# Fifteen quarter products for six tiles of fc1's second half, and new paces for the convolutions, in a two-block image kernel

## The chip, the cores and the metric

The kernel runs on one core of one Trainium2 chip. All arithmetic is in 32-bit floats. The metric is the device time of one execution in microseconds (us); the median over the runs counts.

The engines are TensorE (PE in the profile, PEld for its weight loads), VectorE (DVE), ScalarE (ACT), GpSimd (POOL) and SyncE (SP). Each engine takes its own instructions in the order in which they were issued to it. PE writes its results into PSUM banks, which VectorE and ScalarE read.

## The reference

The input is 8 images of 384 channels and 32 x 32 positions, so 1024 tokens. Each goes through two blocks; what follows is the arithmetic with the set-up left out.

```python
# block 0: attention and MLP, 8 heads of 48, on tokens (N = 1024, C = 384)
xn  = layernorm(xf, eps=1e-5) * g1 + beta1
q, k, v = split(xn @ w_qkv.T + b_qkv)
out = softmax(q @ k.T * 48**-0.5) @ v
x1  = out @ w_proj.T + b_proj + xf
xn2 = layernorm(x1, eps=1e-5) * g2 + beta2
h   = gelu(xn2 @ w_fc1.T + b_fc1)            # 384 -> 1536
y   = x1 + h @ w_fc2.T + b_fc2               # 1536 -> 384
# block 1: 7 x 7 depthwise convolution, MLP with global response norm
z   = depthwise_conv(y, dw_w, pad=3) + dw_b
z   = layernorm(z, eps=1e-6) * ln_w + ln_b
z   = gelu(z @ w1 + b1)                      # 384 -> 1536
gx  = sqrt(sum over positions of z**2); nx = gx / (mean(gx) + 1e-6)
z   = gamma * (z * nx) + gbeta + z
out = y + z @ w2 + b2                        # 1536 -> 384
```

## The kernel before, in words

**Layout.** Channels lie on the 128 partitions, so 384 channels are 3 tiles and 1536 hidden channels are 12 (HT). Tokens run along the free axis, and a matmul takes a half of them (512 columns, NH) at a time. A product of one 128 x 128 weight block with 512 columns is two matmul instructions in the trace. The images are called 0 to 7 here.

**One image after another.** For each image the program issues q and k (L549), attention (scores L664, products L684, the softmax reciprocals `average` L634 to L651, `proj` L606), the layer norm behind it (L413 to L451, its sums over channels as matmuls with ones at L380 and L394), fc1 and fc2 in `mlp`, and the convolution of block 1 (L998). Block 1's two matmul stages of the image before (L338 and L358, `grn_up` and `grn_down`) run on PE while VectorE does the convolution taps of this one. The last image is split by halves instead (`mlp_by_halves`), and its convolution (`last_convolution`) runs in two parts, image rows 0 to 13 and 13 to 32. Its matmuls come in three pieces of 416, 288 and 320 tokens (`last_up` L1168, `grn_down_straight` L1124).

**The order is written out by hand.** There is no scheduler. An object `flow` keeps a plan clock in microseconds: each matmul adds to it (`flow.pe(U)`, 0.857 for a product of 512 columns), and work for the other engines is written as Python generators that yield how long to wait. When the plan clock passes the due time of a generator, its next instructions are issued, between two matmuls. A generator spawned as "paced" keeps to its own times; another counts on from when it was called. `flow.finish` issues all the rest of one at once. So the plan decides only the order of issue on each engine, and semaphores decide when an instruction runs.

**The convolution.** `convolution` issues one tap (one multiply-add of VectorE over a whole channel tile, 1.16 us in the trace) after another, with a pace in plan microseconds. In images 0 to 6 a second generator, `help_convolution`, does 7 of the 49 taps of each channel tile on ACT and POOL (L1019, L1020), and while it works on a tile, VectorE leaves that one alone. The layer norm of the convolution's output follows when both are done.

**fc1.** `mlp` calls `gelu_half` (L768) for each of 12 tiles of hidden channels, first for the first half of the tokens, then for the second. A tile is three products of 512 columns into one of four single PSUM banks (`linear_half` L351) and a gelu on ScalarE (L370) from the bank into the hidden array `hid`. During the first half, after tile 3, the rest of attention and the layer norm of the second half's tokens are issued; the second half starts when that norm is finished. In the second half VectorE has nothing to do for fc1.

**fc2.** `by_thirds` (from L822) takes the 3 x 3 blocks of the weights by 15 products in place of 18, with sums of weight blocks (`FORMS`) made once, in image 0, by `forms` in `prepare` and stored in DRAM (`s_fc2`, `s_w2` for block 1). Its first sums over `hid` are differences of two halves, made by `difference` (L785 negates on ScalarE, L786 adds by a DMA on POOL's queue) during fc1's second half, after its tiles 3 and 5.

**Weights and banks.** Weights come through a ring of 9 buffers of 128 x 768, loaded by SP's queue in a fixed plan; `weights.used` gives a buffer back and starts the next load (L279). SP's queue also moves the softmax reciprocals to where `average` multiplies by them. PSUM has four single banks (`ps_o`) and two double ones (`ps_s`), each set handed out in turn.

Of the kernel before, what the change touches and what calls it, by code (L numbers as in the profile page):

```python
# [51 lines left out]
P = 128  # L52
# [12 lines left out]
CM = 2  # L65
NC = HT // CM
U = 0.857
HELPED = 7
SCALE = HD ** -0.5
EPS0, EPS1, GRN_EPS = 1e-5, 1e-6, 1e-6  # L70
# [81 lines left out]
def block_kernel(  # L152
# [25 lines left out]
    flow = Flow()  # L178
    quiet = []
    s_fc2 = dram.tile([P, len(FORMS), 4 * P], F32, tag="s_fc2", bufs=1, name="s_fc2")  # L180
    s_w2 = dram.tile([P, len(FORMS), 4 * P], F32, tag="s_w2", bufs=1, name="s_w2")
    s_qk = dram.tile([P, CT, 4 * P], F32, tag="s_qk", bufs=1, name="s_qk")
    s_w1 = dram.tile([P, HT // 2, 4, P], F32, tag="s_w1", bufs=1, name="s_w1")

    def half(h):
        return slice(h * NH, (h + 1) * NH)
# [103 lines left out]
    def chunk(w, c):  # L290
        return w[:, c * 6 * P : (c + 1) * 6 * P]
# [1 line left out]

    RAW = ("A11", "A12", "A21", "A22", "A31", "A32")

    def plan_fc1(tag):
        return [((f"fc1_{tag}", c), chunk(wfc1, c)) for c in range(NC)]

    def plan_fc2(tag):
        return [((f"fc2_{tag}", a), chunk(wfc2, c)) for c, a in enumerate(RAW)]  # L300
# [1 line left out]
    def block_of(w, m, k):  # L302

        at = ((m - 1) * HT + 4 * (k - 1)) * P
        return w[:, at : at + 4 * P]
# [8 lines left out]
    def plan_fc2_fast(tag):  # L314
        return plan_thirds(f"fc2_{tag}", wfc2, s_fc2)
# [467 lines left out]
    def difference(dst, more, less):  # L783

        nc.scalar.mul(dst, less, -1.0)  # L785
        nc.gpsimd.dma_start(out=dst, in_=more, accum_op=ALU.add)  # L786
# [5 lines left out]
    def add_first(xt, r, n, bank):  # L792
        dst = xt[:, r, half(n)]
        nc.vector.scalar_tensor_tensor(dst, bank, col("bfc2", r), dst, ALU.add, ALU.add)

    def mlp(b, xt, xn, weights, tag, ln, rest, before_fc2=None, behind_ln=None):

        hid = one.tile([P, HT * N], F32, tag="big", name=f"hid_{b}").rearrange("p (m n) -> p m n", m=HT)
        e = [three.tile([P, 2, NH], F32, tag="p", name=f"fc2_e_{b}_{i}") for i in range(2)]
        wa = f"fc1_{tag}"  # L800
        flow.finish(ln)
        for m in range(HT):
            gelu_half(hid, m, 0, xn, weights, wa, f"fc1_{b}")
            if m == 3 and rest:
                rest()
                slow = 1.2 if b == 1 else 1.0
                ln = flow.spawn(layernorm(xt, xn, 1, eps0, "g2", f"ln2_{b}", True, slow=slow))
                behind_ln(ln)
        flow.finish(ln)
        for m in range(HT):  # L810
            gelu_half(hid, m, 1, xn, weights, wa, f"fc1_{b}")
            if m % CM == CM - 1:
                weights.used(wa, m // CM)
            if m in (3, 5):
                two_tiles = hid[:, m - 3 : m - 1, :]
                difference(e[(m - 3) // 2], two_tiles[:, :, half(0)], two_tiles[:, :, half(1)])
        if before_fc2:
            before_fc2()
        bias = lambda r: col("bfc2", r)
        by_thirds(xt, hid, e, True, weights, f"fc2_{tag}", bias, lambda r, n: pad_half(xt, r, n), f"fc2_{b}")  # L820
# [458 lines left out]
    def prepare(weights, aside):  # L1279
# [17 lines left out]
        def load_blocks(w, name, *which):  # L1297
            t = one.tile([P, CT, N], F32, tag="acc", name=name).rearrange("p c n -> p (c n)")
            parts = []
            for j, (m, k) in enumerate(which):  # L1300
                parts.append(t[:, j * 4 * P : (j + 1) * 4 * P])
                nc.gpsimd.dma_start(out=parts[j], in_=block_of(w, m, k))
            return parts

        def spare(name):
            return three.tile([P, NH], F32, tag="res", bufs=4, name=name)
# [4 lines left out]
        def add(dst, x, y):  # L1311
            nc.vector.tensor_tensor(dst, x, y, ALU.add)

        def forms(name, w, store):
            def keep_form(i, t):
                nc.gpsimd.dma_start(out=store[:, i, :], in_=t)

            a11, a12, a31, a33, a13, a23 = load_blocks(w, f"{name}_a", (1, 1), (1, 2), (3, 1), (3, 3), (1, 3), (2, 3))
            x, y, z = (spare(f"{name}_{k}") for k in "xyz")
            yield 16.0  # L1320
            add(a23, a23, a33)
            add(a11, a11, a12)
            keep_form(6, a11)
            sub(a31, a31, a11)
            keep_form(0, a31)
            yield 2.0
            add(x, a11, a13)
            sub(x, x, a23)
            keep_form(8, x)
            nc.vector.scalar_tensor_tensor(y, a11, -1.0, a33, ALU.mult, ALU.subtract)  # L1330
            keep_form(5, y)
            yield 2.0
            sub(z, a23, a12)
            keep_form(11, z)
            sub(a13, a13, a12)
            sub(a13, a13, a33)
            keep_form(13, a13)
            yield 2.0
            nc.vector.tensor_scalar(a12, a12, -1.0, None, ALU.mult)
            keep_form(12, a12)  # L1340
            nc.vector.tensor_scalar(a23, a23, -1.0, None, ALU.mult)
            keep_form(14, a23)
            a21, a22, a31, a32, a33, a12 = load_blocks(w, f"{name}_b", (2, 1), (2, 2), (3, 1), (3, 2), (3, 3), (1, 2))
            x, y = spare(f"{name}_v"), spare(f"{name}_w")
            nc.gpsimd.dma_start(out=x, in_=block_of(w, 2, 3))
            yield 25.0
            add(x, x, a33)
            sub(y, a22, x)
            keep_form(7, y)
            add(a12, a12, a21)  # L1350
            add(a12, a12, a31)
            keep_form(9, a12)
            yield 2.0
            add(a22, a21, a22)
            sub(a33, a33, a22)
            keep_form(2, a33)
            add(a22, a22, a31)
            keep_form(4, a22)
            add(a32, a32, a22)
            keep_form(1, a32)  # L1360
# [61 lines left out]
            nc.gpsimd.dma_start(out=s_w1[:, :, int(key[1]) - 1, :], in_=t[:, j])  # L1422
        yield from shift_through_w2()
        yield from forms("w2", w2, s_w2)

    def first_values(xn):

# [10 lines left out]
    def main():  # L1438
# [17 lines left out]
        plan = plan_fc1(0) + plan_fc2_fast(0) + plan_qk(1)  # L1456
        for b in range(1, B):
            if b < B - 1:
                plan += plan_fc1(b) + plan_fc2_fast(b)
            else:  # L1460
                for h in range(2):
                    plan += plan_fc1(f"{b}_{h}") + plan_fc2(f"{b}_{h}")
            plan += plan_w1(b - 1, b < B - 1)
            if b == B - 1:
                plan += plan_w1(f"{b}_0", False)
            plan += plan_w2(b - 1, b < B - 1)
            if b < B - 1:
                plan += plan_qk(b + 1)
# [61 lines left out]
        def last_convolution(h, ct, ln=None):  # L1530
            if ct < 0:
                conv_norm(B - 1, ln)
                next_norms(B - 1)
                return
            ready[h].append(ct)
            if ct == 0:
                rows = (LAST[0].stop // W, H) if h else (0, LAST[0].stop // W)
                conv = convolution(last, 0.86 if h else 0.66, (), *rows, ready[h])
                state["conv"] = flow.spawn(after(state["conv"], conv), paced=True)
                if h == 0:  # L1540
                    state["norm_a"] = flow.spawn(after(state["conv"], last_norm(LAST[0], 2.6)))

        for b in range(B):
# [22 lines left out]
            flow.finish(state["norm3"])  # L1566
            if b < B - 1:
                y, gx = grn_up(b - 1, acc, weights, b - 1)
                start_conv(b, 1.6 if b == B - 2 else 1.65, (26, 2.1), (27, 9.0), (35, 4.4))
                scale = flow.spawn(grn_scale(b - 1, gx, weights, b - 1, y))  # L1570
                next_values(b + 1)
                flow.finish(scale)
                quiet.append("w2")
                grn_down(b - 1, y, xt, weights, b - 1, b - 1)
                quiet.clear()
                xt = load_x(b + 1, "x")
            else:

                norm_b = flow.spawn(after(state["conv"], last_norm(LAST[1], 1.0)))
                norm_c = flow.spawn(after(norm_b, last_norm(LAST[2], 1.2)))  # L1580
                y, gx = grn_up_straight(b - 1, acc, weights, b - 1)
                scale = flow.spawn(grn_scale(b - 1, gx, weights, b - 1))
                flow.finish(state["norm_a"])
                sums = small.tile([P, CT, HT], F32, tag="gx_last", bufs=1, name="gx_last")
                y_last = places()
                last_up(last, y_last, 0, sums, weights)
                flow.finish(scale)
                halves = lambda k, part: y[:, k, part]
                blocks = [(r, half(n)) for r in range(CT) for n in range(2)]
                args = b - 1, halves, kept[b - 1], weights  # L1590
                grn_down_straight(*args, b - 1, b - 1, blocks[:-1])
# [147 lines left out]
```

## Time and profile before

| | |
|---|---|
| Median of 7 runs | 3304.57 us (3303.79 to 3309.61) |
| Profiled execution, its own time | 3305.85 us |
| Its span | 3304.1 us |
| Granted TensorE clock, mean | 0.996 |
| PE busy | 3273.6 us (99%), 14296 matmuls |
| DVE busy | 2396.5 us (73%) |
| ACT busy | 1606.1 us (49%) |
| POOL busy | 484.3 us (15%) |
| fc1's 1152 matmul instructions (L351) | 502.3 us busy |
| Convolution taps of images 0 to 6 (L998 into acc) | 861, 1157 ns each |
| Convolution taps of image 7 (L998 into wqkv) | 288, 697 ns each |

Times in the profile are microseconds of one profiled execution, a mean duration where marked ns. "L351" is line 351 of the kernel, often a helper's. In the order of work, a row has the start, the busy time, engine, line, operation, output and inputs, shape, and the number of equal instructions in a row; a bracket holds the idle time before it and what ended that. PE's matmuls overlap, so the distance between starts, not the duration of one, is what a matmul takes of PE's time.

### The profile page before, as it was taken

Reading aid. Unit: us, or ns where it says so; the run is one execution under the profiler, and the core shown is the slowest. Engines: PE = TensorE matmul, PEld = TensorE weight load, DVE = VectorE, ACT = ScalarE, POOL = GpSimd, SP = SyncE. Lnnn points to the kernel's source line nnn. Section 1 sums busy time; section 2 is a strip of 40 time slices with the busy share of each in tenths; the row PEclk is TensorE's granted clock in tenths of the full one; section 3 lists DMA queues with packets and bytes.
Section 4 is the critical chain, followed back from the end, with each engine's and each line's share of the span. In section 5 each row is a group of like instructions: output and inputs, shape, how many; then the busy total and the mean of one; then the engine's idle time right before and its main releaser. Section 6 shows DMA issues by size and latency. Waiting matters only on the chain.

```text
span 3304.1 us, 38767 instructions
## 1 busy us (share of the span) xinstructions
PE 3273.6 (99%) x14296; PEld 1413.6 (43%) x14296; DVE 2396.5 (73%) x3186; ACT 1606.1 (49%) x2194; POOL 484.3 (15%) x569
## 2 busy tenths in 40 slices
PE   8999999999999999999999999999999999999998
PEld 4344434443344433444344443444434444344455
DVE  4444787887857978579786797767876788879840
ACT  2542663446634375353662636526474355623541
POOL 2121210112110121101211012110221112100000
PEclk9999999999999999999999999999999999999999
DMA  5336732647345563536536373273842647333231
GB/s 197 112 107 144 149 70 71 156 111 158 57 96 143 133 128 56 127 114 164 95 58 143 102 187 71 53 169 89 187 72 59 178 89 173 70 78 89 69 96 43
DMA packets 199109, 368.73 MB, mean 112 GB/s; under 512 B 40768, under 2 KB 46784, under 8 KB 198528
## 3 DMA queue, kind: packets, MB, share of 16 engines
q0 software_dynamic: 80896, 158.63, 26.3%
q1 hardware_dynamic: 117728, 206.83, 21.0%
q8 instruction: 115, 1.88, 0.2%
q10 hardware_dynamic: 288, 0.71, 0.1%
q14 instruction: 82, 0.67, 0.1%
HBM read 187.03 MB, written 34.60 MB: 67 GB/s over the span
## 4 chain that ended last, share of the span: by engine, by line
PE 89%; DMA 1%; issue 0%; DVE 0%; ACT 0%; POOL 0%; POOLq 0%; ACTq 0%; DVEq 0%
PE fc L351 15%; PE s L664 11%; PE o L684 11%; PE h L358 10%; PE fc_p L358 10%; PE o_p L358 9%; PE qk L358 6%; PE o L1124 4%; PE proj L606 3%; PE v L592 3%; PE h_last L1168 2%; PE h L338 2%; PE ln_var L394 1%; PE ln_sum L394 0%; DMA ln_sq<-ln_sq 0%
## 5 line engine op out<-in xcount | busy, mean ns | idle before, releaser
L998 DVE SCALAR_TENSOR_TENSOR acc<-pad,vec,acc 128x870 f32<-128x870 f32 (+7 forms) x861 | 964.2, 1157 | 8.9 <-DMA acc<-tap 4.3
L673 ACT ACTIVATE p<-s 128x1024 f32<-128x1024 f32 x512 | 524.4, 1025 | 285.0 <-PE s L664 278.0
L664 PE MATMUL s<-qk 48*64 48x512 f32 x4096 | 546.1, 592 | 0.2 <-ACT qk L505 0.2
L684 PE MATMUL o<-p,v 64*64 64x512 f32 x4096 | 543.4, 590 | 0.0
L351 PE MATMUL fc<-xn,fc 128*128 128x512 f32 x1152 | 502.3, 594 | 0.0
L1020 POOL DMA_DIRECT2D acc<-tap x294 | 253.5, 878 | 1211.9 <-ACT tap L1019 772.2
L351 PEld LDWEIGHTS fc<-xn,fc 128*128 128x128 f32 x1152 | 217.5, 190 | 280.6 <-issue 268.8
L358 PE MATMUL fc_p<-hid,fc 128*128 128x512 f32 x728 | 319.4, 596 | 0.0
L370 ACT ACTIVATE hid<-fc,bfc_f 128x512 f32<-128x512 f32 x192 | 131.4, 686 | 343.8 <-PE fc L351 343.7
L684 PEld LDWEIGHTS o<-p,v 64*64 64x64 f32 x4096 | 165.4, 133 | 278.4 <-issue 270.1
L664 PEld LDWEIGHTS s<-qk 48*64 48x64 f32 x4096 | 161.6, 133 | 277.7 <-issue 222.9
L358 PE MATMUL o_p<-y,w 128*128 128x512 f32 x624 | 270.9, 592 | 0.0
L1069 DVE TENSOR_TENSOR y<-h,y 128x512 f32<-128x512 f32 x288 | 197.1, 690 | 89.8 <-PE h L358 75.2
L1019 ACT ACTIVATE tap<-pad,vec 128x512 f32<-128x512 f32 x294 | 213.0, 734 | 13.7 <-DMA acc<-tap 13.6
L358 PEld LDWEIGHTS fc_p<-hid,fc 128*128 128x128 f32 x728 | 138.3, 191 | 177.6 <-issue 173.5
L358 PE MATMUL h<-acc,w_A 128*128 128x512 f32 x432 | 207.3, 595 | 0.0
L358 PEld LDWEIGHTS o_p<-y,w 128*128 128x128 f32 x624 | 118.0, 190 | 148.7 <-issue 132.0
L998 DVE SCALAR_TENSOR_TENSOR wqkv<-pad,vec,wqkv 128x377 f32<-128x377 f32 (+24 forms) x288 | 177.4, 697 | 0.6
L625 DVE TENSOR_TENSOR attn<-o,attn 128x512 f32<-128x512 f32 x64 | 44.2, 690 | 164.2 <-ACT attn L623 164.2
L790 ACT COPY pad<-x 128x512 f32<-128x512 f32 x48 | 30.2, 635 | 250.0 <-DVE x L856 194.1
L549 DVE TENSOR_TENSOR qk<-qk,qk 128x512 f32<-128x512 f32 x168 | 114.5, 689 | 37.2 <-PE qk L358 28.6
L592 PE MATMUL v<-wqkv,xn 128*128 128x384 f32 x384 | 128.8, 493 | 0.0
(311 smaller groups left out, 3751.5 us busy)
## 6 DMA issues: line engine op xcount, KB each, us to landing
acc<-tap POOLq DMA_DIRECT2D x294, 256.0 KB, 3.4
w_A<-in_w SPq DMA_DIRECT2D x72, 384.0 KB
fc<-s_fc SPq DMA_DIRECT2D x91, 256.0 KB
hid<-hid POOLq DMA_DIRECT2D x42, 512.0 KB, 7.1
fc<-in_wfc SPq DMA_DIRECT2D x54, 384.0 KB
w<-s_w SPq DMA_DIRECT2D x78, 256.0 KB
y<-y POOLq DMA_DIRECT2D x36, 512.0 KB, 7.2
kept<-x SPq DMA_DIRECT2D x8, 1536.0 KB
```

Of the source, the lines that this page charges most:

```text
L351: nc.tensor.matmul(out=ps, lhsT=lhsT(k), rhs=rhs(k)[:, half(h)], start=(k == 0), stop=(k == nk - 1))
L358: nc.tensor.matmul(out=bank, lhsT=lhsT, rhs=rhs, start=k == 0, stop=k == len(pairs) - 1)
L370: nc.scalar.activation(dst, src, function, **kw)
L592: nc.tensor.matmul(out=ps[:, :C], lhsT=xn[:, k, t * P : (t + 1) * P], rhs=wv_sb[:, k, :], start=(k == 0), stop=(k == CT - 1),)
L664: nc.tensor.matmul(out=s[64 * i : 64 * i + 64, j, :], lhsT=kT[64 * j : 64 * j + HD, m, k0 : k0 + 64], rhs=qT[64 * j : 64 * j + HD, m, half ...
L673: nc.scalar.activation(p, s, AF.Exp)
L684: nc.tensor.matmul(out=outs[i][64 * j : 64 * j + 64, :], lhsT=v[keys, t, at : at + 64], rhs=p[keys, j, :], start=(t == 0), stop=(t == KT - 1),
L998: nc.vector.scalar_tensor_tensor(dst, window, tap, dst, ALU.mult, ALU.add)
L1019: nc.scalar.mul(t.rearrange("p (h w) -> p h w", w=W), window, tap)
L1020: nc.gpsimd.dma_start(out=acc[:, ct, half(h)], in_=t, accum_op=ALU.add)
L1069: nc.vector.tensor_tensor(dst, bank, part, ALU.add)
L1124: nc.tensor.matmul(out=ps, lhsT=tiles[k], rhs=y(k, part), start=(k == 0), stop=(k == HT - 1))
```

## The change

In images 1 to 6 the second half of the tokens in fc1 is taken in another way for hidden tiles 6 to 11. These six are two groups of three tiles (`FAST = 2`). Within a group the 3 x 3 weight blocks (three tiles by three channel tiles) meet the second half of the tokens cut into two quarters of 256 columns, and the six blocks of the result are made from 15 products of 256 columns, where there were 18, by the same forms as in fc2.

- `quarter_sums` makes ten sums of quarters of the tokens on VectorE before the first group, behind the layer norm.
- `fc1_group` issues the 15 products into seven banks (y, t, z, v single; x and three others from the double ones), with a second product added onto the same bank five times, and 13 operations of VectorE and four copies of ScalarE that put the results together. The gelus of a group, on `hid` in place, are kept in the list `late` and issued among the next group's or the next tiles' products.
- The second half goes: tiles 0 and 1, group 0, tile 2, group 1, tile 3, then 4 and 5. The first half begins with tiles 6 to 11, whose weight chunks are given back there. The differences for fc2 are issued with group 0 (tiles 0 and 1) and after tile 3.
- The weights' forms for fc1 (`s_fc1`, 15 forms of two groups) are made and stored in image 0, after those of w2.
- The paces of the convolutions change: 1.65 to 1.58 in images 1 to 5, 1.6 to 1.55 in image 6, and in image 7 0.66 to 0.56 for the first part and 0.86 to 0.72 for the second.

```diff
+FAST = 2
...
+    def plan_fc1(tag, fast=False):
+        order = [*range(NC // 2, NC), *range(NC // 2)] if fast else range(NC)
+        return [((f"fc1_{tag}", c), chunk(wfc1, c)) for c in order]
+
+    def plan_fc1_fast(tag):
...
+            for i, (k, l) in enumerate(((0, 6), (6, 12), (12, 15))):
+                plan.append(((f"fc1f_{tag}", g, i), s_fc1[:, g, k:l, :].rearrange("p i o -> p (i o)")))
...
+    def quarter_sums(xn, t):
+        b11, b12, b21, b22, b31, b32 = (xn[:, k, quarter(n, NH)] for k in range(3) for n in range(2))
+        e, f, h, e2, g, f2, h2, g2, f3, d = t
+        minus = ((e, b11, b12), (f, e, b21), (h, e, b31), (f3, f2, g2), (d, g2, b31))
+        plus = ((e2, h, b12), (g, b22, f), (f2, f, b12), (h2, h, b32), (g2, g, b32))
+        for n, (dst, x, y) in enumerate(minus[:3] + plus + minus[3:]):
+            nc.vector.tensor_tensor(dst, x, y, ALU.subtract if n < 3 or n > 7 else ALU.add)
+            if n % 2:
+                yield 1.0
+
+    def fc1_group(hid, group, xn, sums, weights, wname, name, late):
...
+        def product(i, ps, more=False):
+            w = weights.at(wname, group, i // 6)[:, i % 6, :]
+            nc.tensor.matmul(out=ps, lhsT=w, rhs=right[i], start=not more, stop=True, skip_group_check=more)
+            flow.pe(U / 2)
...
+        y = product(6, bank("y"))
+        nc.scalar.copy(c11, y)
+        t = product(2, bank("t"))
+        nc.scalar.mul(c21, t, -1.0)
+        x = product(0, bank("x", True))
+        nc.scalar.copy(n16, x)
+        z = product(10, bank("z"))
+        product(5, y, True)
+        lately()
+        product(1, t, True)
+        v_ = product(12, bank("v"))
+        nc.scalar.copy(c12, v_)
+        op(n16, y, n16)
+        x = product(3, bank("u", True))
+        op(c32, x, n16)
+        op(c32, c32, z, ALU.subtract)
+        x = product(4, bank("w", True))
+        lately()
+        op(c12, c12, z, ALU.subtract)
+        op(n17, x, n16)
+        op(c31, t, n17)
+        x = product(14, bank("q", True))
+        op(c21, x, c21)
+        product(11, v_, True)
+        op(c11, v_, c11)
+        lately()
+        product(7, z, True)
+        product(13, y, True)
+        op(c12, y, c12)
+        product(8, x, True)
+        op(c11, x, c11)
+        product(9, v_, True)
+        op(n17, v_, n17, ALU.subtract)
+        op(c22, z, n17)
+        op(c21, c21, n17)
...
+        late += [gelu(2), gelu(1), gelu(0)]
...
+        fast = FAST if isinstance(b, int) and b > 0 else 0
...
-        for m in range(HT):
+        for n in range(HT):
+            m = (n + HT // 2) % HT if fast else n
             gelu_half(hid, m, 0, xn, weights, wa, f"fc1_{b}")
...
+                making = flow.spawn(after(ln, quarter_sums(xn, sums), 1)) if fast else None
...
+            plain(0)
+            plain(1)
+            late.append(lambda: difference_of(0))
+            fc1_group(hid, 0, xn, sums, weights, f"fc1f_{tag}", f"fc1_{b}", late)
+            plain(2)
+            fc1_group(hid, 1, xn, sums, weights, f"fc1f_{tag}", f"fc1_{b}", late)
+            plain(3)
+            difference_of(1)
+            for m in (4, 5):
+                plain(m)
+                late.pop(0)()
+            late.pop(0)()
...
         yield from forms("w2", w2, s_w2)
+        yield from forms("fc1", wfc1, s_fc1)
...
-                conv = convolution(last, 0.86 if h else 0.66, (), *rows, ready[h])
+                conv = convolution(last, 0.72 if h else 0.56, (), *rows, ready[h])
...
-                start_conv(b, 1.6 if b == B - 2 else 1.65, (26, 2.1), (27, 9.0), (35, 4.4))
+                start_conv(b, 1.55 if b == B - 2 else 1.58, (26, 2.1), (27, 9.0), (35, 4.4))
```

The names in `fc1_group` with a 1 or 2 behind a c are blocks of the result: "c32" is the third tile's second quarter. `n16` and `n17` are intermediate sums, kept in the two halves of one buffer.

## The prediction

> **What bounds the kernel now.** I read the page first, then the waits of TensorE (PE), then the order of work on PE and VectorE (DVE) in fc1's second half and in the last image. The page says that PE is the path:
>
> ```profile
> PE 3273.6 (99%) x14296; PEld 1413.6 (43%) x14296; DVE 2396.5 (73%) x3186; ACT 1606.1 (49%) x2194; POOL 484.3 (15%) x569
> PE 89%; DMA 1%; issue 0%; DVE 0%; ACT 0%; POOL 0%; POOLq 0%; ACTq 0%; DVEq 0%
> ```
>
> PE idles 30.5 us of 3304.1, most of it at the start. So a matmul taken away is worth its full time, and any new wait of PE costs its full time. The question is what PE will wait for, and DVE at 73% is the candidate. PE in the last image:
>
> ```profile
> 3054.27 0.86 PE L380 MATMUL ln_sum<-ln_a,ones 128*128 128x416 f32 x2
> ...
> 3071.12 24.20 PE L338 MATMUL h<-acc,w_A 128*128 128x512 f32 x56
> 3095.15 7.15 PE L1168 MATMUL h_last<-wqkv,w_A 128*128 128x416 f32 x20
> ...
> 3173.88 0.75 PE L380 MATMUL ln_sum<-ln_a,ones 128*128 128x288 f32 x2 [1.70 <-DVE ln_a L416]
> 3177.07 0.75 PE L380 MATMUL ln_var<-ln_sq,ones 128*128 128x288 f32 x2 [2.44 <-DVE ln_sq L437]
> 3179.44 6.79 PE L1168 MATMUL h_last<-wqkv,w_A 128*128 128x288 f32 x16 [1.62 <-DVE wqkv L451]
> ...
> 3186.61 6.95 PE L1168 MATMUL h_last<-wqkv,w_A 128*128 128x288 f32 x28
> 3193.40 0.70 PE L380 MATMUL ln_var<-ln_sq,ones 128*128 128x320 f32 x2
> ```
>
> Starts give the price of a matmul instruction (each product is two): 512 columns (3095.15 - 3071.12) / 56 = 0.4291 us, 288 columns (3193.40 - 3186.61) / 28 = 0.2425. On the line through both, 256 columns cost 0.2158. The brackets are the waits at the tail of the last convolution: 5.76 us. DVE in the second half of fc1 (image 2, 936.7 to 968.8) and in the last image:
>
> ```profile
> 931.09 11.73 DVE L998 SCALAR_TENSOR_TENSOR acc<-pad,vec,acc 128x930 f32<-128x930 f32 x10
> 942.85 0.69 DVE L413 TENSOR_TENSOR ln_a<-acc 128x512 f32<-128x512 f32 x1
> 943.58 0.69 DVE L416 TENSOR_TENSOR ln_a<-ln_a,acc 128x512 f32<-128x512 f32 x1
> 944.18 0.69 DVE L413 TENSOR_TENSOR attn<-acc 128x512 f32<-128x512 f32 x1
> ...
> 3034.06 10.18 DVE L998 SCALAR_TENSOR_TENSOR wqkv<-pad,vec,wqkv 128x403 f32<-128x403 f32 x19
> 3044.13 1.74 DVE L996 TENSOR_SCALAR wqkv<-pad,vec 128x608 f32<-128x608 f32 x2
> 3045.76 0.61 DVE L413 TENSOR_TENSOR ln_a<-wqkv 128x416 f32<-128x416 f32 x1
> 3046.40 0.59 DVE L416 TENSOR_TENSOR ln_a<-ln_a,wqkv 128x416 f32<-128x416 f32 x1
> ```
> ```profile
> 936.70:968.80 32.10, 32.10 (x82) 13.79 (x81) 12.06 (x16) 11.84 (x18) 4.11 (x4) 1.00 0.39 82
> 2950.00:3044.20 94.20, 94.20 (x231) 40.60 (x230) 91.46 (x171) 25.60 (x36) 2.64 (x4) 1.00 0.34 91
> ```
>
> Columns of the last two: length, then busy time of PE, PEld, DVE, ACT (ScalarE), POOL. In the second half DVE is busy for 12.06 of 32.10 us and ACT for 11.84; nothing there makes DVE wait for PE, so it runs ahead of its plan. In 2950 to 3044, the first part of the last convolution, DVE is full: 91.46 of 94.20.
>
> **Matmuls saved.** A group of three tiles by two quarters took 18 instructions of 0.4291 = 7.72 us and takes 30 of 0.2158 = 6.47: 1.25 less. Two groups in images 1 to 6: 12 x 1.25 = **-15.0 us**. [...] The 288-column row, with a load of 190 ns in each 242, lies where streaming alone puts it, so the sum keeps 15.0; the bounds are 15.0 and, if 256 columns cost as much as 288, 360 x 0.0267 = 9.6 less, which is 5.4.
>
> **What the groups make PE wait for.** DVE had no work of fc1; now it has 13 operations of 256 columns a group, on banks that PE writes again within the group. Behind a product that waits, every later matmul is queued, so each wait counts in full. Price: 512 columns take 0.69, and starts lie 0.60 apart (944.18 - 943.58), or 0.73 where one needs the one before; less 256 columns at 0.96 a ns, which is 0.267: 0.34 and 0.46. Eight and five of these are 5.0 us, beside 6.47 of PE. That fits, just. But DVE takes its queue in order, and the planner puts convolution taps of 1.165 us between. By the code's own pacing the last taps of image 2 stand at plan times 899.5 to 914.1, the second half starts at 901.2 and group 0 (after two plain tiles of 2.57) at 906.3. The pace 1.58 for 1.65 leaves nine taps for ten and ends them at 911.5, no earlier: the last ones wait for the helped channel tile, not for the pace. So seven are done before group 0 needs DVE and two lie inside it. Followed from the group's start (a product 0.43, 0.20 until its result is seen, 0.16 from DVE to PE): c32 is made at 3.65; product 14, which takes the double bank that c32 is read from, waits 0.4 for it; the tap then holds "c12 minus z" back to 5.6, and product 7 on z waits 1.1; product 8 waits 0.3; the second tap holds c12 back to 8.6, and the next plain tile, whose bank is y's, waits 1.0. That is 2.7; group 1, with no tap inside, keeps 0.4 + 0.2 of it: 3.3 an image, 2.3 if only one tap falls inside; I take 2.8, for images 2 to 6. Image 1 keeps the old pace and has four taps in each group (its taps run to plan time 530, the second half to 535): DVE has 4 x 1.165 + 5.0 = 9.7 for the 9.05 of a group and a plain tile, and the same walk gives 3.8. Together 5 x 2.8 + 3.8 = **+17.8**; bounds 3.4 (0.56 an image, no tap ever in the way) and 27. The ten quarter sums (about 3.8 us, DVE) fit before group 0: image 2's DVE has its last xn at 931.1 and group 0 wants its first operation near 944. ScalarE's 24 more copies and moved gelus lie in its 20 us of idle there: 0.
>
> **Moved DMAs.** difference_of(1) moves from 952.9 to about plan tile 10; issue 1.2 and landing near 5.5 us put it 3 us ahead of its product in fc2: 0, and PE pays what it lands later. Chunks 3 to 5 are given back in the first half, so one load of 384 KB goes out on SP ahead of the last softmax reciprocals r (issued 902.2, used 906.0 to 906.7, wanted by proj near 908.3). At queue 1's rate (206.83 MB in 21.0% of the span, 298 GB/s) it takes 1.3 plus 0.35 to issue, against 1.5 of slack: 0.2 x 6 = **+1.0** (0 to 9). The s_fc1 forms add some 20 DVE operations of 0.43 and 28 DMAs on POOL to image 0, after w2's, which end at 242 while the tile they use is wanted at about 340: **+0.5** (0 to 3).
>
> **The denser last convolution.** Its part 1 (147 taps, pace 0.66 to 0.56) ends 147 x 0.10 = 14.7 us earlier in the plan, and with it the layer norm behind it, whose sums PE takes in its order. DVE cannot follow: it is full, and reaches the end at most 1.8 earlier (a tap and one operation less ahead). Before, ln_a was ready at 3046.99 and PE summed it at 3054.27, slack 7.3; now 7.3 - 14.7 + 1.8 - 1.5 (a tap or two of part 2 get in front) = -7.1, so PE waits 7.1 in all there, about 2.3 of it already at the acc norm's variance. Between that sum and the next one, ten taps of part 2, 7.1 us, lie in DVE's queue before it subtracts the mean, while the plan gives it 0.8: the variance's sum waits another 5.7. Part 2 (0.86 to 0.72, 106 us planned for 104 of taps and 9 of other work) ends at 3155 for 3171, and its norm costs 3.1 where 5.76 and some 0.7 at acc's variance went before. 7.1 + 5.7 + 3.1 - 6.5 = **+9.4**; bounds -5.8 (those waits go and none comes) and +14.
>
> **Sum.** -15.0 + 17.8 + 1.0 + 0.5 + 9.4 = +13.7. The profiled execution took 3305.85 (span 3304.1 and 1.75 around it), 1.3 over the median; taken off the median: 3304.57 + 13.7 = **3318.3**.
>
> **Rivals.** *DVE has room where I count none* (faster). One mechanism, DVE's place in its queue against PE's: if it gets to the groups' operations and to the last norm's sums about 7 us earlier than I walk it, the group waits fall to 3.4 and the last image's go: -15.0 + 3.4 + 1.5 - 5.8 = -15.9, 3288.7. For it: DVE idles 20 us in the second half. Against: the 94 us without a gap. It decides where ln_sum's slack stays above 0. *The last convolution costs nothing, the groups what I say*: -15.0 + 17.8 + 1.5 = +4.3, 3308.9; for it, the tail's 5.76 us of waits do shrink. *DVE falls behind for good*: with a tap more in each group (1.165 x 12 = 14) the sum is 3332; for it image 1's 9.7 against 9.05, against it that taps end at 911.5. *It doesn't save matmul time* (256 costs 288's price): +9.6, 3327.9.
>
> **How the numbers follow.** Forecast 0.56, in 3311 to 3328; the two dearer cases 0.04 each, to 3333. Costless last convolution: 0.12, within 0.2% (6.6 us, about what a measurement of this kernel can tell from no change). DVE with room: 0.24, anywhere from 3280 to 3298. Slower by over 0.2%: 0.64; within: 0.12; faster: 0.24. The range leaves out the lower two thirds of the fast case (0.16) and 0.04 at the top: 3292 to 3333.
>
> **What would show it.** Right: PE's matmul count up by 12 x 12 = 144 (14296 to 14440); 256-column starts 0.216 apart; PE waiting about 3 us a second half on DVE, in group 0 more than in group 1; ln_sum of 128x416 waiting on DVE ln_a; the 288-column waits gone or moved. Wrong: second halves 2.5 us shorter (groups free), no wait at ln_sum, a new wait on fc_e or on weights, or PE waits above 25 us in the six images.

## The result, and the profile after

The changed kernel takes 3313.73 us (median of 15 runs, 3311.3 to 3316.45), the kernel before 3304.57 (35 runs): a ratio of 1.0026, 95% interval 1.0019 to 1.0033. It is slower by 9.2 us; the forecast was 13.7 slower. Its profiled execution took 3312.3 us, with a span of 3310.5.

The page of the changed kernel, in the two rows that were shown of before:

```profile
PE 3266.9 (99%) x14440; PEld 1452.3 (44%) x14440; DVE 2478.7 (75%) x3422; ACT 1617.4 (49%) x2240; POOL 504.6 (15%) x597
DVE 7%; PE 4%; DMA 0%; issue 0%; ACT 0%; DVEq 0%
```

There are 144 matmuls more, as forecast, and PE is busy for 6.7 us less; yet the span is longer, so PE waits more. The chain that ended last now leads back to VectorE's taps (its shares add up to 11%: it is followed back through the last image only). PE in the last image, where before had three waits, of 1.70, 2.44 and 1.62 us, all at the 288-column norm:

```profile
2975.86 5.39 PE L361 MATMUL fc<-xn,fc 128*128 128x512 f32 x12 [2.09 <-DVE acc L433]
2982.27 10.66 PE L361 MATMUL fc<-xn,fc 128*128 128x512 f32 x24 [1.03 <-DVE x L804]
...
3049.07 1.08 PE L390 MATMUL ln_sum<-ln_a,ones 128*128 128x416 f32 x2 [4.28 <-DVE ln_a L426]
3049.94 17.24 PE L348 MATMUL h<-acc,w_A 128*128 128x512 f32 x36
3070.59 1.76 PE L390 MATMUL ln_var<-ln_sq,ones 128*128 128x416 f32 x2 [3.42 <-DVE ln_sq L447]
3072.14 40.41 PE L348 MATMUL h<-acc,w_A 128*128 128x512 f32 x92
...
3160.19 0.72 PE L390 MATMUL ln_sum<-ln_a,ones 128*128 128x288 f32 x2 [0.15 <-DVE ln_a L426]
```

The waits have moved from the 288-column norm to the 416-column one, over 100 us earlier, and two new ones stand in fc1 of the last image's second half. The starts of the same work on PE, before and after, say what each stage costs (each line is the difference of two starts in the trace):

| stage on PE | before, us | after, us | difference |
|---|---|---|---|
| start to fc2 of image 0 | 272.97 | 272.08 | -0.9 |
| fc2 of image 0 | 59.20 | 62.01 | +2.8 |
| fc1 and second proj of image 1 | 71.34 | 73.09 | +1.7 |
| fc1 after proj in images 2 to 6, each | 54.44 | 54.21 | -0.23 |
| image 7, from the second proj to the end of fc2 | 112.53 | 116.02 | +3.5 |
| first stage of image 6's block 1, with the 416-column norm's sums in it | 63.20 | 74.63 | +11.4 |
| first piece of image 7's block 1 | 25.36 | 26.89 | +1.5 |
| from there to the end of the other pieces | 99.80 | 90.77 | -9.0 |

What lies between these stages adds -0.2 in all, so PE is 9.7 us later at the last stage. The profile ends only 6.4 us later (3310.5 for 3304.1): from the start of that last stage to the end of the program the changed kernel takes 3.4 us less. Its matmuls there take the same time; behind them GpSimd's last long instruction, the DRAIN at the program's end that the other engines' last ones come after, is shorter. Before and after (shortest, middle and longest of three in ns, then the starts):

```profile
L1735 POOLq DRAIN  x3: 51/107/6679, 3296.6 to 3303.8; - x3
L1886 POOLq DRAIN  x3: 51/107/3739, 3305.6 to 3309.9; - x3
```

The longest one falls by 2.9 us, and the instruction just ahead of it on GpSimd (INC_SWDGE_SEM) by 0.7. So the stages account for 6.4 of the medians' 9.2; the profiled run of before is 1.3 us above its median and that of after 1.4 below, which is the rest. The first row is not the change's: between the profiles below, with the same code there, it differs from before's by between 1.3 us less and 1.0 more.

Then a group. PE and VectorE in group 0 of image 2, in order of time:

```profile
949.03 0.59 PE L838 MATMUL fc_w<-fc_t,fc1f 128*128 128x256 f32 x2
949.71 0.70 PE L838 MATMUL fc_q<-hid,fc1f 128*128 128x256 f32 x2
950.25 0.59 PE L838 MATMUL fc_v<-hid,fc1f 128*128 128x256 f32 x2
951.56 0.70 PE L838 MATMUL fc_z<-hid,fc1f 128*128 128x256 f32 x2 [0.72 <-DVE hid L843]
952.10 0.59 PE L838 MATMUL fc_y<-xn,fc1f 128*128 128x256 f32 x2
952.69 0.70 PE L838 MATMUL fc_q<-xn,fc1f 128*128 128x256 f32 x2
953.23 0.59 PE L838 MATMUL fc_v<-hid,fc1f 128*128 128x256 f32 x2
```
```profile
949.69 0.42 DVE L843 TENSOR_TENSOR hid<-hid,fc_z 128x256 f32<-128x256 f32 x1
950.03 1.15 DVE L1129 SCALAR_TENSOR_TENSOR acc<-pad,vec,acc 128x899 f32<-128x899 f32 x1
951.09 0.41 DVE L843 TENSOR_TENSOR hid<-hid,fc_z 128x256 f32<-128x256 f32 x1
```

A row of PE is one product, two instructions. A group's 15 products go to eight banks (the list of the change has seven), and seven of them (not five) are added onto one that is there. Where nothing waits, products start 0.43 apart (952.10 less 951.56 has 0.11 more, since it follows a wait). Product 7 on z starts at 951.56, not at 950.68: VectorE read that bank for "c12 minus z" at 951.09, behind the tap of 950.03. Before q there is 0.25 more than 0.43, before the second q 0.16. These are the waits that were walked through in the prediction. Note that the bracket says 0.72 where the start is 0.88 late, and that the waits before q have no bracket: matmul ends in the page are modelled, so starts are the measure.

### The profile page after: what moved, and what is told of

Same layout as the page of the kernel before. It is cut to its first block, busy times and chain, and to the rows that moved or that the text cites. A ratio compares the mean times of both kernels' runs of the same rounds, so it can differ in the third digit from the quotient of the medians.

```text
span 3310.5 us, 39506 instructions
## 1 busy us (share of the span) xinstructions
PE 3266.9 (99%) x14440; PEld 1452.3 (44%) x14440; DVE 2478.7 (75%) x3422; ACT 1617.4 (49%) x2240; POOL 504.6 (15%) x597
## 5 line engine op out<-in xcount | busy, mean ns | idle before, releaser
L1129 DVE SCALAR_TENSOR_TENSOR acc<-pad,vec,acc 128x899 f32<-128x899 f32 (+8 forms) x861 | 963.6, 1157 | 12.5 <-DMA acc<-tap 9.2
L361 PE MATMUL fc<-xn,fc 128*128 128x512 f32 x936 | 411.9, 594 | 3.1 <-DVE acc L433 2.1
L694 PEld LDWEIGHTS o<-p,v 64*64 64x64 f32 x4096 | 172.6, 133 | 270.5 <-issue 258.2
L361 PEld LDWEIGHTS fc<-xn,fc 128*128 128x128 f32 x936 | 176.4, 190 | 227.4 <-issue 208.2
L380 ACT ACTIVATE hid<-fc,bfc_f 128x512 f32<-128x512 f32 x156 | 106.6, 686 | 340.0 <-PE fc L361 339.9
L1129 DVE SCALAR_TENSOR_TENSOR wqkv<-pad,vec,wqkv 128x290 f32<-128x290 f32 (+21 forms) x288 | 177.4, 699 | 0.7
L368 PEld LDWEIGHTS h<-acc,w_A 128*128 128x128 f32 x432 | 80.6, 190 | 108.0 <-issue 95.0
```

The source lines that it names most:

```text
L361: nc.tensor.matmul(out=ps, lhsT=lhsT(k), rhs=rhs(k)[:, half(h)], start=(k == 0), stop=(k == nk - 1))
L368: nc.tensor.matmul(out=bank, lhsT=lhsT, rhs=rhs, start=k == 0, stop=k == len(pairs) - 1)
L380: nc.scalar.activation(dst, src, function, **kw)
L694: nc.tensor.matmul(out=outs[i][64 * j : 64 * j + 64, :], lhsT=v[keys, t, at : at + 64], rhs=p[keys, j, :], start=(t == 0), stop=(t == KT - 1),
L1129: nc.vector.scalar_tensor_tensor(dst, window, tap, dst, ALU.mult, ALU.add)
```

## The experiments

Each ran on one chip with the kernel before beside it, whose median is given too. The stages in each profile were compared as in the table.

**The changed kernel once more.**

> The changed kernel itself, unaltered, so that the three others have it beside them. 3313.7 us within 2, and in its profile the same stages: image 0's fc2 2 to 4 us longer than before's 59.2, each second half of fc1 in images 2 to 6 0.23 us shorter than before's, image 1's 1.7 us longer, the last image 7.4 us longer.

3313.77 us beside 3303.55, ratio 1.0030 (1.0020 to 1.0041): 10.2 slower. The stages came out as expected: +3.5 in image 0's fc2, +1.6 in image 1, -0.23 in each of five images, +7.4 from image 7's fc1 to its last stage.

**The last convolution as before.**

```diff
-                conv = convolution(last, 0.72 if h else 0.56, (), *rows, ready[h])
+                conv = convolution(last, 0.86 if h else 0.66, (), *rows, ready[h])
```

> The changed kernel with the last image's two paces put back to 0.66 and 0.86, all else as changed. Theory: the denser last convolution makes TensorE wait 9.1 us more in part 1 (two waits of 4.3 and 3.4 us at the 128x416 sums, each with some 1.6 us of half clock behind it) and about 3.5 us more in fc2 of the last image's first half, and saves 9 us at the 128x288 sums: 7.4 us net. Without it 3313.7 - 7.4 = 3306.3 us, with no wait over 1 us at the 128x416 sums. Rival one, the denser convolution costs nothing and the groups are what costs: 3313 us or more. Rival two, it gains something: above 3314 us.

3305.98 beside 3303.85, ratio 1.0003 (0.9994 to 1.0012); the last image takes 0.15 us less than before's. That is 7.8 below the changed kernel, or 7.0 when each is taken against the kernel before beside it (9.2 and 2.1 us slower). So 7 to 8 of the 9.2 us are the last convolution's. The groups with all else make the other 2.1, which these runs cannot tell from nothing; by the profile it is 5.5 us on PE less 3.4 at the program's end.

**Only the first part as before** (0.72 and 0.66).

> The changed kernel with only the first part's pace put back to 0.66; the second part keeps 0.72. Theory: the cost is all in the first part, the gain all in the second. The 128x416 sums do not wait, and the 288-column norm's 9 us (waits of 1.7, 2.4 and 1.6 us and the slow matmuls behind them) shrink by half or more: 3306.3 less 4 to 8, so 3298 to 3302 us. Rival: VectorE has no time to give in either part, so what the second part does earlier, the first part's norm or ScalarE pays later: 3305 us or more, as with both paces put back.

3298.64 beside 3303.85, ratio 0.9982 (0.9973 to 0.9991). The last image takes 7.6 us less than before's; no wait stands at the 416-column sums, and 0.9 us is left at the 288-column one. The second part alone gains.

**The second part's pace in the kernel before.**

> The kernel before with one number altered: the second part's pace of the last convolution 0.72 for 0.86. Theory: what the second part gains is apart from the groups: 7.6 us less in the last image (the waits of 1.7, 2.4 and 1.6 us at the 288-column norm and the slow matmuls behind them), 3296 us. Rival: VectorE has that time only because the groups' kernel reaches the last image with more of its taps done: 3302 us or more.

3296.56 beside 3304.59, ratio 0.9977 (0.9968 to 0.9986), 7.2 of it in the last image. The gain needs nothing of the groups. PE in this kernel's tail:

```profile
3157.21 0.75 PE L380 MATMUL ln_sum<-ln_a,ones 128*128 128x288 f32 x2 [0.91 <-DVE ln_a L416]
3157.80 7.03 PE L1124 MATMUL o<-y,w_A 128*128 128x512 f32 x16
3164.66 0.65 PE L380 MATMUL ln_var<-ln_sq,ones 128*128 128x288 f32 x2
```

The norm is now early enough that its sums lie among image 6's last matmuls, which cover its chain; in the rows of before only the norm itself was left to do there.

**Only the second part as before** (0.86 and 0.56).

> The changed kernel with only the second part's pace put back, 0.56 and 0.86: the fourth of the four pairs of paces. Theory: the first part's pace alone costs about 15 us (3.5 in fc2, 11.4 at the two 128x416 sums) whatever the second part's, and the second part's alone gains 7.6: 3306 + 15 = 3321 us, with the waits at the 288-column norm back. Rival: the first part's finishing earlier lets the second part start earlier, so that the 288-column waits are gone without a denser second part: about 3313, as with both.

3310.25 beside 3303.68, ratio 1.0020 (1.0011 to 1.0029). A miss: the last image costs 3.4, not 15.

```profile
3046.09 1.30 PE L390 MATMUL ln_sum<-ln_a,ones 128*128 128x416 f32 x2 [3.15 <-DVE ln_a L426]
3047.19 17.02 PE L348 MATMUL h<-acc,w_A 128*128 128x512 f32 x36
3065.58 0.97 PE L390 MATMUL ln_var<-ln_sq,ones 128*128 128x416 f32 x2 [1.38 <-DVE ln_sq L447]
...
3185.13 5.12 PE L1299 MATMUL h_last<-wqkv,w_A 128*128 128x288 f32 x20 [1.27 <-DVE wqkv L461]
```

The two parts do not add. A first part that ends earlier in the plan lets the second begin earlier, and that alone takes most of the 288-column waits away (the rival). And the variance's wait is 1.38 here against 3.42 with both dense. VectorE's taps ahead of "minus the mean" and ahead of the sum of squares, in this kernel:

```profile
3049.04 6.59 DVE L1129 SCALAR_TENSOR_TENSOR wqkv<-pad,vec,wqkv 128x551 f32<-128x551 f32 x9
3055.55 1.58 DVE L433 SCALAR_TENSOR_TENSOR wqkv<-ln_sum,wqkv 128x416 f32<-128x416 f32 x3
3057.04 7.28 DVE L1129 SCALAR_TENSOR_TENSOR wqkv<-pad,vec,wqkv 128x589 f32<-128x589 f32 x10
```

There are 9 and 10, where the changed kernel has 10 and 12 (its rows stand further below): three taps, 2.2 us, about the difference of the waits. By the starts, the second part's denser pace is worth -7.6 us with 0.66 before it and costs 4.0 (7.4 less 3.4) with 0.56.

**No tap within a group.** While a group's products are issued, the convolution's generator only waits.

```diff
-            if not left:
-                yield 1.0
+            if not left or held:
+                yield 0.5 if held else 1.0
...
+        held.append(group)
         y = product(6, bank("y"))
...
+        held.clear()
```

> The changed kernel with no convolution tap issued while a group's products are issued; the taps go behind the group. Theory: the tap between two of the group's VectorE operations is what product 7 waits for. Images 2 to 6: group 0 falls from 8.08 us to about group 1's 7.15 us, 0.9 each; image 1, with taps in both groups, from 4.2 us of waits to about 1.4. Together 5 x 0.9 + 2.8 = 7.3: 3306.4 us. Rival: the group's own chain of VectorE operations is what makes it wait: within 1 us of 3313.7. Rival two: the held taps come out later and delay the norm behind the convolution, whose sums then wait in fc2: 3310 to 3314 us with new waits at the sums of 64x512.

3311.6 beside 3303.85, ratio 1.0023 (1.0014 to 1.0032): 7.75 slower where the changed kernel is 10.2, so a gain of 2.5 and not 7.3. The mechanism is there; group 0 of image 2 takes 7.01 us (947.23 to 954.24) for 8.08:

```profile
951.37 0.70 PE L839 MATMUL fc_q<-hid,fc1f 128*128 128x256 f32 x2
951.90 0.59 PE L839 MATMUL fc_v<-hid,fc1f 128*128 128x256 f32 x2
952.33 0.59 PE L839 MATMUL fc_z<-hid,fc1f 128*128 128x256 f32 x2
952.76 0.59 PE L839 MATMUL fc_y<-xn,fc1f 128*128 128x256 f32 x2
```

Product 7 on z no longer waits. Images 2 to 6 take 1.25 us less than before's each, where the changed kernel took 0.23 less. Image 1 gives its gain back: its held taps put off the norm behind the convolution, whose variance then waits 0.83 in fc2 and slows what follows, and the image ends 1.4 us behind before's where the changed kernel's was 1.7. By the profiles the gain is 5.4; why the medians show 2.5 was not settled (image 0's fc2, which the edit does not touch, took 4.0 us more than before's in this profile).

**Another order inside a group.**

```diff
         op(c12, c12, z, ALU.subtract)
-        op(n17, x, n16)
-        op(c31, t, n17)
-        x = product(14, bank("q", True))
-        op(c21, x, c21)
         product(11, v_, True)
+        q = product(14, bank("q", True))
+        op(c21, q, c21)
         op(c11, v_, c11)
+        op(n17, x, n16)
+        op(c31, t, n17)
...
-        product(8, x, True)
-        op(c11, x, c11)
+        product(8, q, True)
+        op(c11, q, c11)
```

> The changed kernel with the order inside a group altered: product 11 goes ahead of 14, and VectorE takes c21 and c11 ahead of n17 and c31. Theory: what is left of a group's wait without a tap (0.35 at product 14 and 0.2 to 0.3 at product 8, each with 0.10 of slower start in it) is the order of VectorE's chain against the two double banks, and goes: group 1 falls from 7.15 to 6.5 us. In group 0 product 7 still waits for the tap, and takes over part of what product 14 waited: 8.08 to about 7.8. With image 1 about 5 x 0.95 + 1 = 5.7 less: 3308 us. Rival: VectorE has no room at all there, and each wait comes back at product 7 or 9: within 1.5 us of the changed kernel.

3312.25 beside 3303.55, ratio 1.0025 (1.0014 to 1.0036): 1.5 better than the changed kernel, not 5.7.

```profile
951.00 0.59 PE L838 MATMUL fc_q<-hid,fc1f 128*128 128x256 f32 x2
952.67 0.70 PE L838 MATMUL fc_z<-hid,fc1f 128*128 128x256 f32 x2 [1.07 <-DVE hid L843]
```

The wait at q is gone and product 7 waits that much longer: it needs VectorE behind the tap, whatever PE does ahead of it. Images 2 to 6 gain 0.26 each. The rival held while a tap lies in the group.

**The convolutions' paces of images 1 to 6 as before.**

> The changed kernel with the convolution paces of images 1 to 6 put back to 1.65 and 1.6. The prediction gave the denser pace nothing, since the last taps wait for the helped tile. Theory now: put back, the last taps come 2.6 plan us later, so one more of them lies within the groups, and the norm's first sums move into group 1: 0.7 to 1 us more in images 2 to 6, 3317 to 3319 us. Rival: the same, within 1 us of the changed kernel, since the taps there are late for the helped tile anyway.

3314.55 beside 3303.55, ratio 1.0029 (1.0019 to 1.0039), within 0.8 of the changed kernel. The rival held in the medians, which show the denser pace of these images to be worth nothing. By the starts it is worth a little: fc1 after proj in images 2 to 6 takes 1.7 us more in all than in the changed kernel.

**The forms of fc1 later in image 0.**

```diff
-            yield 25.0
+            yield 48.0 if w is wfc1 else 25.0
```

> The changed kernel with one pause of the forms of fc1 in image 0 lengthened from 25 to 48 plan microseconds, so that the second lot of their stores goes out on GpSimd's queue behind the norm's four additions and fc2's four, not between them. Theory: those six stores hold up GpSimd's queue, since each waits for VectorE there, and the two sums of the next image's norm come 1.4 and 3.1 us late; image 0's fc2 falls from 62.0 to about 59.3 us and the whole by 2.8: 3310.9 us. Rival: it is the traffic of the forms (loads and stores together), which stays: 3313 us and the same waits. Rival two: the stores delay the first tap behind them, whose tile they use: the time moves to image 0's block after fc2, 3313 us.

3309.66 beside 3303.85, ratio 1.0018 (1.0009 to 1.0027): 5.8 slower where the changed kernel is 10.2. GpSimd's queue in the changed kernel (start, duration of the issue, the wait ahead of it):

```profile
291.68 0.72 POOL L1459 DMA_DIRECT2D s_fc<-fc_w  x1 [1.42 <-DVE fc_w L1448]
292.48 0.69 POOL L1459 DMA_DIRECT2D s_fc<-fc_b  x1
294.40 1.40 POOL L1459 DMA_DIRECT2D s_fc<-fc_b  x2 [1.24 <-DVE fc_b L1448]
297.71 0.69 POOL L1459 DMA_DIRECT2D s_fc<-fc_b  x1 [1.90 <-PE ln_sum L404]
298.27 2.59 POOL L996 DMA_DIRECT2D hid<-hid  x2
```

The first of the two additions to hid in the last row was issued earlier in the kernel before:

```profile
292.56 1.22 POOL L865 DMA_DIRECT2D hid<-hid  x1 [2.26 <-PE fc_p L358]
```

Stores that wait for VectorE hold back the additions of 512 KB to hid, of which four follow. The last of these lands at 314.6 (311.1 before), so they run on beside the norm's two, of which the first, issued at 311.4 (311.3), lands after 5.7 us (3.4 before). The variance's sum waits for it:

```profile
317.27 1.08 PE L404 MATMUL ln_var<-ln_sq,ones 64*64 64x512 f32 x4 [3.13 <-DMA ln_sq<-ln_sq]
```

With the stores later, that row and the next:

```profile
315.19 1.07 PE L404 MATMUL ln_var<-ln_sq,ones 64*64 64x512 f32 x4 [0.37 <-DMA ln_sq<-ln_sq]
317.61 1.97 PE L404 MATMUL ln_var<-attn,ones 64*64 64x512 f32 x4 [1.34 <-DMA attn<-attn]
```

The wait went, and a smaller one stands at the other half. In that one profile the stage as a whole gained nothing (+2.8 again), since PE ran slowly behind the second wait (granted clock 0.50 from 317.6 to 321.0). So the move of the wait is shown, and the 4.4 us of the medians are not traced to it.

**The forms alone.** Everything undone but the forms, which nothing then uses.

> The changed kernel with everything undone but the forms of fc1 that image 0 makes and stores (no later image uses them): fc1 by whole tiles, all paces as before. Theory: what image 0's fc2 pays in the profiles of the changed kernel (2.8 to 3.8 us) is the price of the forms, as GpSimd's queue and the transfers beside the norm's two additions: 3 to 4 us over the kernel before, about 3307. Rival: image 0 varies by itself from run to run, and the forms cost nothing: within 1 us of the kernel before.

3305.43 beside 3303.68, ratio 1.0005 (0.9996 to 1.0014): 1.75 us, not clear of nothing. Its profile shows image 0's fc2 5.2 us longer; over the nine profiles with the forms in the change's place that stage was between 0.4 shorter and 5.2 longer, 3.2 longer on average, and over the three with the later place 0.8; without forms it took 59.2 and 59.6 in two. The 1.75 us have the shorter end of the program in them: in this profile PE is 4.7 us later at the last stage and the end takes 3.3 less. The shorter end comes with the forms: it is 3.2 to 3.4 us shorter in all twelve profiles that have them, this one among them, and the same as before's in the one other run that has not (the second part's pace in the kernel before). So the forms cost PE some 3 us on average, more or less from run to run, and give back about as much at the end. Why GpSimd's DRAIN is shorter with their 28 DMAs on its queue is not shown.

**Together**: the first part's pace as before, forms later, taps held, the other order.

> Four alterations of the changed kernel together: the first part's pace of the last convolution back to 0.66, the second lot of fc1's forms later, no tap issued within a group, and the altered order inside a group. Theory, from the stages: with the first part's pace alone 3298.6; the held taps take 1.0 from each of images 2 to 6 and little from image 1 (its norm comes late): 5; the order inside a group takes 0.54 from each of 12 groups: 6.5; the forms 0 to 3. Together 3284 to 3288 us. Rival: the parts overlap, since with the taps held back the same wait would go by either, and the held taps delay the norm: 3292 us or more.

3288.53 beside 3303.55, ratio 0.9958 (0.9944 to 0.9971). In a group only 0.27 us of waits are left; images 2 to 6 gain 1.77 each against before, the last image 7.6, the program's end 3.2; image 1 loses 5.0.

**Together, and image 1 by whole tiles.**

> The kernel with the four alterations together, with the groups left out of image 1, whose fc1 goes by whole tiles as before. Theory: in the four together image 1 loses 5.0 us against before (the held taps put off the norm behind the convolution, whose second sum TensorE then waits for in fc2), images 2 to 6 gain 1.95 each, the last image 7.6, and image 0 loses 2 to 3. Without image 1's 5.0: 3288.5 - 5.0 = 3283.5 us. Rival: image 1's loss is of the later images' weights or of image 0 and stays: 3288 us.

3284.8 beside 3303.68, ratio 0.9946 (0.9933 to 0.9960): 18.9 us faster than before and the best of all. Image 1's loss was its own. What PE still waits for in the whole of it (three rows of 0.2 to 0.5 us left out):

```profile
PE ln_sum L391 <- DVE ln_a L427: 11.2, 5, 6.1
PE ln_sum L405 <- DMA ln_a<-ln_a: 1.0, 1, 1.0
PE b L250 <- DVE b_f L1533: 0.5, 2, 0.3
...
```

Of the 11.2 us, 10.3 are the start of the kernel.

## Why the prediction was right, and where it was not

**Direction and size**: 13.7 us slower forecast, 9.2 measured. The forecast held as the sum of a saving that was real, waits that ate it, and a last convolution that cost more than it gave. That it came within 4.5 us is in part luck: the group waits and the last convolution were priced 2.2 and 2.0 too high, the moved load 1.0 too high and the forms some 2 too low, and the 3.4 us less at the program's end were in no term.

**Matmuls saved, -15.0: right.** Starts 945.58, 946.01, 946.44 of products of 256 columns are 0.43 apart, 0.2158 an instruction, as the line through 512 and 288 columns gave. The price goes with the columns down to there: of 512 columns' 0.4291, 288/512 is 0.2414 (0.2425 measured) and 256/512 is 0.2146, with a weight load of 0.19 in each. 256 columns at 288's price is out.

**Group waits, +17.8: 15.6 measured.** Images 2 to 6 lost 2.27 each to waits (2.5 saved, 0.23 left), image 1 4.2 (forecast 2.8 and 3.8). In group 0 product 14 lost 0.35 (0.4), product 7 0.99 (1.1), product 8 0.26 (0.3), each with 0.10 in it for a slower start behind a wait; group 1 lost 0.68 (0.6). Two taps lay inside, as forecast. The walk's prices held: VectorE takes 0.69 for 512 columns and 0.42 for 256, so 0.27 less (0.267); its operations in the group start 0.33 to 0.34 apart (0.34), 0.46 where one needs the one before (949.23 to 949.69; 0.46); and u's product, over at 949.03 by the starts, is read at 949.23 (0.20). The step that failed here is the plain tile behind the group, which was to wait 1.0 for y's bank and waits for nothing:

```profile
953.66 0.59 PE L361 MATMUL fc<-xn,fc 128*128 128x512 f32 x1
953.91 0.42 DVE L843 TENSOR_TENSOR hid<-fc_y,hid 128x256 f32<-128x256 f32 x1
```

It starts before VectorE reads y for the last time, so it has got another bank. The walk with that wait came to 3.3 an image and without it to 2.3, which is what was measured; the 2.8 was taken between them because a tap might fall outside, and none did. With the taps held, product 7's wait went; that it is the tap is shown.

**Moved DMAs**: r's later load, +1.0, cost nothing: from the start of fc1 to the end of the second proj, where r is wanted, images 1 to 6 take 18.1 us each before and after. The forms in image 0, +0.5 with 3 as the end, were mis-sized: 2.8 in the profile's fc2 of image 0, 3.2 on the average of nine; by the medians 1.75 with the forms alone, which has the shorter end in it, and 4.4 by putting them later. They were priced as work of VectorE and as loads past their time; what the rows show is GpSimd's queue, where a store that waits for VectorE holds the additions to hid behind it and these then slow the norm's.

**The denser last convolution, +9.4: 7.4 by the starts, 7.8 by undoing it.** The terms, in order. What comes before the 416-column sums, where VectorE is late with acc's norm: 2.3 forecast, 3.5 measured. The 416-column sum: 4.8 forecast (7.1 less 2.3), 4.4 measured. The variance's wait, 5.7 from ten taps in front of "minus the mean": 3.6 measured. The ten taps are there on VectorE, and twelve more in front of the sum of squares:

```profile
3051.90 7.37 DVE L1129 SCALAR_TENSOR_TENSOR wqkv<-pad,vec,wqkv 128x551 f32<-128x551 f32 x10
3059.18 1.59 DVE L433 SCALAR_TENSOR_TENSOR wqkv<-ln_sum,wqkv 128x416 f32<-128x416 f32 x3
3060.67 8.67 DVE L1129 SCALAR_TENSOR_TENSOR wqkv<-pad,vec,wqkv 128x589 f32<-128x589 f32 x12
```

The kernel before has nearly as many in the same two places:

```profile
3047.72 6.59 DVE L998 SCALAR_TENSOR_TENSOR wqkv<-pad,vec,wqkv 128x551 f32<-128x551 f32 x9
3056.67 7.29 DVE L998 SCALAR_TENSOR_TENSOR wqkv<-pad,vec,wqkv 128x589 f32<-128x589 f32 x10
```

They cost nothing there, since PE took the sum at 3054.27, when VectorE was through with the nine. The denser plan has PE ask after 16 matmuls of the stage instead of 52, which is 15.4 us sooner, and counted from the start of that stage VectorE has ln_a ready only 3.8 us sooner (11.2 for 15.0). So the mechanism is as forecast: PE asks much earlier and VectorE cannot follow.

Two things were not in the sum: 3.3 us of slow matmuls behind the two waits, and 1.5 us in the first piece, where PE waits for ScalarE. In the second profile of the changed kernel the slow matmuls cost 1.5 us more and the first piece nothing, so there PE's own lateness seems to hide the wait for ScalarE; the last image costs 7.4 in both. And the tail was mis-sized: 9.0 saved, where 6.5 less 3.1 was forecast. Before's waits had cost more than the brackets' 5.76, which leave out 2.7 us of slow matmuls behind them and what the modelled ends hide; and after the change next to nothing of them is left, where 3.1 was forecast.

**Rivals.** "DVE has room" would have meant no wait at the 416-column sums, and there are two. "The last convolution costs nothing" would have left the change at 3308.9, and undoing the convolution gave 3305.98: its price for the groups and the rest was 2.9 too high, its premise wrong. "DVE falls behind for good" did not come.

## What to carry to other kernels

A saving on the engine that bounds the kernel is only as large as the slack of whoever must read its results: 15 us of matmuls were saved and 15.6 lost in waits. About half of the loss in images 2 to 6 came of two taps of 1.15 us that stood in VectorE's queue between operations of 0.4, and half of the rest came of the order inside the group. Holding unrelated work back for the few microseconds of a tight exchange kept 1.77 of 2.5 us an image once the exchange's own order was mended too. A denser pace moves work of an engine that is already full only in the plan: what depends on it is asked for earlier and waited for (here 15.4 us sooner, and ready 3.8 sooner), so each stretch wants its own pace, and two stretches that follow each other are tried together. Stores that wait for another engine do not belong in a queue that a norm's additions have to pass (here 3.13 us of wait at the variance's sum; 0.37 and 1.34 at its two halves with the stores later). And the time between PE's last matmul and the end of the program belongs in the sum: here it moved by 3.4 us, and no stage of PE shows it.

## What the runs showed of the hardware that was not expected

**Some waits cost more than their length.** Behind the waits of 4.3 and 3.4 us at the 416-column sums PE ran at about half its clock for some 3.3 us:

```profile
3049.00:3053.40 4.40, 4.33 (x7) 1.96 (x8) 3.70 (x7) 2.79 (x4) 0.00 (x0) 0.61 0.49 195
3053.40:3057.00 3.60, 3.60 (x10) 1.59 (x9) 3.60 (x6) 1.77 (x2) 0.00 (x0) 1.00 0.70 235
3070.00:3073.70 3.70, 3.10 (x4) 1.52 (x5) 3.70 (x6) 1.26 (x3) 0.00 (x0) 0.54 0.00 0
```

The granted clock (the third number from the end of a row) is 0.61 and 0.54 there and 1.00 on either side. Matmuls of 512 columns start 0.85 apart for 0.43, and each of the two waits costs 1.6 us on top. How long it lasts is not fixed: in the second profile of the changed kernel the same wait of 3.4 us is followed by 6.4 us of it (granted clock 0.52 from 3073.2 to 3079.7), which cost 3.1. In the kernel before, the three waits of 1.7, 2.4 and 1.6 us, with four short matmuls between them, had the same effect, at a granted clock of 0.59 in

```profile
3179.40:3186.00 6.60, 6.56 (x16) 4.81 (x17) 1.74 (x4) 2.44 (x6) 0.00 (x0) 0.59 0.00 0
```

and 2.7 us of cost; the single waits of 2.1 and 1.0 us in fc1 of the last image had none (granted clock 1.00 behind each). Which waits bring it on, and what sets its length, is not shown.

**In the groups, the first matmul behind a wait starts its successor 0.10 us late**: 0.32 to the next for 0.216 at 256 columns (951.56 to 951.88 in group 0), which a group paid at each of its waits.
